# A scheduler that lays Fourier mixes later after their sines, and new shares for its four side chains: a vision-transformer layer on one core

## The chip, the core and the metric

The kernel runs on one core of one Trainium2 chip. The metric is the device time of one execution in microseconds (us), median of the runs of one comparison. The engines of the core are named as the profile names them: PE (TensorE; PEld is its weight loads), DVE (VectorE), ACT (ScalarE), POOL (GpSimd) and SP (SyncE, which here only issues DMAs). They run side by side and wait for each other through semaphores.

## What is computed

Sixteen images of 3 x 512 x 512 pixels are cut into 1024 patches of 768 values each. All numbers are float32.

```
h = patches @ W.T + b                              # tokens, width 256
x = layernorm(h);  q, k, v = split(x @ w_qkv)       # 8 heads of 32
k = sum over f = 1..256 of a_f*sin(f*k) + b_f*cos(f*k)   # element by element
h = h + softmax(q @ k.T / sqrt(32)) @ v @ w_out + b_out
x = layernorm(h)
h = h + mlp(x) + top-2 of 4 experts(x), weighted    # gates: softmax, top 2, softmax again
```

## The kernel before

The 256 Fourier terms of a key are not taken one by one. For a group of 8 rows of keys three tiles of 128 x 1024 are made: two "slow" waves `w` and one "fast" wave `f`. A DMA copies the angles into `w` (a shuffle on DVE copies them into `f`), POOL multiplies each row by its frequency (`turn`, line 953), and ACT takes the sine (line 963). Then PE **mixes**: sixteen matmuls on tiles of 64 x 32 combine the two slow waves with the coefficients (`mix`, line 987). The first eight read wave 0 and the next eight wave 1. DVE multiplies the result by the fast wave (`prod`, line 1001), and a matmul on tiles of 128 x 32 adds up what belongs together (`red`, line 1020). Each image has 32 such groups; all sixteen have 512.

Attention follows two rounds behind: scores on PE (`sT`, line 1085), exponentials on ACT (line 1100), and the weighing of the values on PE with tiles of 128 x 64 (`av`, line 1117). Then come a reciprocal and a product on DVE.

This fixed work is laid out in **rounds**: four groups of keys, and eight blocks of scores of one attention step (a pair of heads, half of the queries). Within a round ACT does twelve sines in one go, then loads the other table, then does eight exponentials: `sine` twice for group 0, twice for group 1, once for each of their fast waves, and the same again for groups 2 and 3. Eight rounds make an image, 130 rounds the whole. I call the stretch from the last `av` matmul of a round to the last mix of the next round the **sine phase**, and the stretch from there to its last `av` the **attention phase**.

All the rest is cut into pieces and fed to four **chains**, Python generators which yield the engine they want next: chain 0 keys, queries and values; chain 1 projection, gates and networks; chain 2 the small work on gate weights; chain 3 tokens and first norm of coming images. On PE nearly all of these pieces run on the full 128 x 128 array.

A planner, executed while the kernel is built, decides in which order the instructions stand on each engine. It keeps a modelled clock for every engine and a modelled time `done` for every result. `begin` gives the earliest start of a fixed step: the engine's clock, or the time of its dependencies plus `LAG` = 0.06. The loop `run` looks at the next fixed step on PE and at the pieces that want PE. A piece is laid if it can start early enough before the fixed step (`then - IDLE`, or `fixed - 2 * SWITCH` where the fixed step would go on in the tiling that PE already has), or if its chain is overdue (`due > 0`) and the fixed step would not go on in that tiling. `due` grows with the modelled cost of fixed PE work: for each chain `PACES` holds a share and a cap, and a piece of the chain takes its own cost off again. Other costs of the model: `SWITCH` = 0.18 for another tiling, a sine 0.96, a mix 0.86.

A mix depends on the sine of its slow wave 0 and on "sine late", which is set to the end of the sine of slow wave 1 less 0.1. The planner's clock decides the order alone: on the chip every instruction still waits on its semaphores.

Of the kernel before, what the change touches and what calls it, by code (L numbers as in the profile page):

```python
# [53 lines left out]


LAG, LANDS, TABLE, PER_COLUMN, SWITCH, IDLE = 0.06, 2.0, 1.28, 1.0 / 600, 0.18, 0.3
PACES = ((0.155, 2), (0.44, 2), (0, 0), (0.178, 2.6))

TILINGS = {"mix": (64, 32), "av": (128, 64), "red": (128, 32)}

@with_exitstack
def plain_path(ctx: ExitStack, tc: tile.TileContext, a: dict, out: bass.AP, verdict: bass.AP):
# [152 lines left out]
    clock = {e: 0.0 for e in (PE, ACT, DVE, POOL, SP)}  # L215
    queues = {e: {} for e in clock}
    done = {}
# [12 lines left out]
    def begin(engine, deps):  # L230

        if any(d not in done for d in deps):
            return None
        return max([clock[engine]] + [done[d] + LAG for d in deps])

    def retile(tiling):

        same = now["tiling"] == tiling
        now["tiling"] = tiling
        return 0.0 if same else SWITCH  # L240

    def together(at, queue):

        (cost, _, key, _), *rest = queues[PE][queue][:2]
        tiling = TILINGS.get(key[0])
        if tiling is None or now["tiling"] == tiling or not rest or rest[0][2][0] != key[0]:
            return at
        then = begin(PE, rest[0][1])
        return at + 2 * IDLE if then is None else max(at, then - cost)
# [6 lines left out]
    def side_tile(name):  # L256

        i = chains[now["chain"]]["bank"] = banks(now["chain"])[0][1]
        return side.tile([P, 512], FP, tag=f"side{i}", name=name)
# [91 lines left out]
    def lay(engine, queue):  # L351
        cost, deps, key, action = queues[engine][queue].pop(0)
        at = begin(engine, deps)
        if engine == PE:
            cost += retile(TILINGS.get(key[0]))
        clock[engine] = at + cost
        done[key] = clock[engine]
        if engine == PE:
            for ch, (pace, most) in zip(chains, PACES):
                ch["due"] = min(ch["due"] + pace * cost, most)  # L360
        action()

    def heads(engine):
        for rank, (name, steps) in enumerate(queues[engine].items()):
            at = begin(engine, steps[0][1]) if steps else None
            if at is not None:
                yield at, rank, name
# [30 lines left out]
    def run():  # L398

        while True:  # L400
            soonest = others(clock[PE])
            fixed = min(heads(PE), default=None)
            then = fixed and together(fixed[0], fixed[2])
            follows = fixed and TILINGS.get(queues[PE][fixed[2]][0][2][0]) == now["tiling"] != None
            pieces = [
# [307 lines left out]
    def gates(b, half, late=False):  # L713
# [20 lines left out]
        now["stream"] += 2 * P  # L734
        now["piece"] = TILINGS["red"]
        yield ACT, 0.25
# [17 lines left out]
    def networks(b, half, late=False):  # L754
# [29 lines left out]
        def second_of_experts(u, e1):  # L784
            yield GO
            ps = side_tile("e2p")
            now["piece"] = TILINGS["av"]
            now["stream"] -= 512
# [397 lines left out]
    for b in range(B):  # L1186
# [6 lines left out]
        late = b == B - 1  # L1193
# [799 lines left out]
```

## Time and profile before

| | before |
|---|---|
| time, median of three runs | 4168.1 us (4166.77 to 4168.17) |
| span of the profiled execution | 4169.3 us |
| PE, ACT, POOL, DVE busy | 97%, 79%, 77%, 68% |
| granted TensorE clock, mean | 0.993 |
| one image in the steady part | 250.6 us |

The last row is the distance between the first PE instructions after the last `av` matmul of one image's rounds and the next one's (1153.84 to 1404.47 us). Matmuls of PE are pipelined and their ends are modelled, so that a PE that stands still inside a group of matmuls is shown as busy. The chain of waits and the timeline tell more than the share.

### The profile page before, as it was taken

To read this page: it belongs to the slowest core of one execution; us is meant where nothing else is said; L and a number is where in the kernel's file an instruction comes from. 1 tells how busy PE (TensorE), PEld (TensorE's weight loads), DVE (VectorE), ACT (ScalarE), POOL (GpSimd) and SP (SyncE) were. 2 spreads that over 40 slices of the span, in tenths; PEclk is the share of its full clock that TensorE was granted. 3 is DMA by queue.
4 is the path that set the end of the run, shared out by engine and by line. 5 is a ranking of instruction groups with operands and counts; after the bars stand their busy time and mean duration, and the time that the engine had idled before them with its cause. 6 is when DMAs were issued, how large, how long until landed. Compare 5 with 4: busy or idle time off the path is not lost.

```text
span 4169.3 us, 67564 instructions
## 1 busy us (share of the span) xinstructions
PE 4027.4 (97%) x22753; PEld 1766.4 (42%) x22753; DVE 2830.2 (68%) x4172; ACT 3286.3 (79%) x3939; POOL 3195.8 (77%) x2323
## 2 busy tenths in 40 slices
PE   6889999999999999999999999999999999999998
PEld 4324344443434445344444444444444444443334
DVE  4667767677676776767767677776767767677652
ACT  2688888788787888878788888788788788888873
POOL 3988877778787887878787787888778787787850
PEclk9999999999999999999999999999999999999999
DMA  7988878888787887978878878887887978878740
GB/s 223 263 241 222 243 200 223 238 218 247 207 232 219 239 235 210 244 211 224 247 209 238 221 225 225 228 241 209 234 228 219 251 211 239 219 211 226 197 138 16
DMA packets 587478, 914.27 MB, mean 219 GB/s; under 512 B 58828, under 2 KB 177524, under 8 KB 587124
## 3 DMA queue, kind: packets, MB, share of 16 engines
q1 hardware_dynamic: 580880, 906.98, 78.7%
q8 instruction: 184, 3.01, 0.3%
q10 hardware_dynamic: 6244, 2.88, 0.3%
q14 instruction: 170, 1.39, 0.1%
HBM read 758.64 MB, written 150.99 MB: 218 GB/s over the span
## 4 chain that ended last, share of the span: by engine, by line
PE 74%; ACT 10%; DVE 6%; DMA 5%; issue 3%; SPq 2%; POOL 1%; ACTq 0%; DVEq 0%; POOLq 0%
PE av L1117 18%; PE sT L1085 11%; PE kan L987 9%; PE tok L263 6%; PE e3p L263 5%; PE red L1020 5%; PE e1p L263 5%; ACT w L963 4%; DMA w<-ud 3%; PE s1p L263 3%; PE q L263 2%; PE v L263 2%; PE proj L263 2%; DVE f L1001 2%; PE k L263 2%
## 5 line engine op out<-in xcount | busy, mean ns | idle before, releaser
L953 POOL TENSOR_TENSOR w<-w,lane 128x1024 int32<-128x1024 int32 x1024 | 1926.1, 1896 | 444.4 <-DMA w<-ud 298.6
L1100 ACT ACTIVATE es<-sT 128x1024 f32<-128x1024 f32 x1024 | 1033.0, 1022 | 550.0 <-PE av L1117 339.8
L953 POOL TENSOR_TENSOR f<-f,lane 128x1024 int32<-128x1024 int32 x512 | 971.0, 1896 | 251.2 <-DVE f L938 157.5
L963 ACT ACTIVATE w<-w 128x1024 f32<-128x1024 int32 x1024 | 1021.1, 1048 | 42.1 <-POOL w L953 39.1
L1117 PE MATMUL av<-es,v 128*64 128x512 f32 x4096 | 965.1, 602 | 1.0 <-DVE rc L1162 1.0
L1143 DVE RECIPROCAL rc<-av 128x256 f32<-128x256 f32 x256 | 434.0, 1730 | 702.6 <-PE av L1117 702.6
L1085 PE MATMUL sT<-q,k 128*128 128x512 f32 x2048 | 691.7, 449 | 42.0 <-DVE f L1001 20.2
L1001 DVE TENSOR_TENSOR f<-kan,f 128x1024 f32<-128x1024 f32 x512 | 608.5, 1218 | 159.8 <-ACT f L963 123.7
L938 DVE STREAM_SHUFFLE f<-src 128x1024 int32<-128x1024 int32 x512 | 673.0, 1353 | 0.7
L987 PE MATMUL kan<-w,coef 64*32 64x512 f32 x8192 | 623.9, 600 | 39.5 <-ACT w L963 35.6
L1085 PEld LDWEIGHTS sT<-q,k 128*128 128x128 f32 x2048 | 346.0, 189 | 440.5 <-issue 219.0
L963 ACT ACTIVATE f<-f 128x1024 f32<-128x1024 int32 x512 | 516.1, 1048 | 2.6 <-POOL f L953 2.6
L1117 PEld LDWEIGHTS av<-es,v 128*64 128x64 f32 x4096 | 258.5, 136 | 563.2 <-issue 498.2
L263 PE MATMUL tok<-wt,x 128*128 128x256 f32 x1536 | 362.3, 387 | 16.9 <-DMA w1s<-in_sW 13.6
L263 PEld LDWEIGHTS tok<-wt,x 128*128 128x128 f32 x1536 | 288.7, 192 | 110.8 <-issue 34.7
L987 PEld LDWEIGHTS kan<-w,coef 64*32 64x32 f32 x8192 | 127.9, 105 | 375.2 <-ACT w L963 222.5
L1020 PE MATMUL red<-f,pack 128*32 128x512 f32 x2048 | 273.6, 604 | 1.5 <-DVE f L1001 1.3
L263 PE MATMUL e1p<-hT,w1e 128*128 128x512 f32 x480 | 233.2, 608 | 0.4 <-ACT e L799 0.4
L462 ACT ACTIVATE hn<-h,less,rstd 128x256 f32<-128x256 f32 x256 | 143.8, 591 | 51.6 <-POOL less L454 51.2
L963 ACT ACT_TABLE_LOAD x128 | 164.2, 1283 | 22.4 <-DMA w<-ud 20.2
L1150 DVE TENSOR_TENSOR aT<-av,rc 32x512 f32<-32x512 f32 x256 | 176.1, 688 | 6.4
L1231 ACT ACT_TABLE_LOAD x128 | 164.2, 1283 | 2.2
(125 smaller groups left out, 3746.7 us busy)
## 6 DMA issues: line engine op xcount, KB each, us to landing
w<-ud SPq DMA_DIRECT2D x2048, 256.0 KB
q<-qd SPq DMA_DIRECT2D x512, 128.0 KB
k<-kd SPq DMA_DIRECT2D x128, 512.0 KB
x<-in_xT SPq DMA_DIRECT2D x128, 384.0 KB
ud<-u SPq DMA_DIRECT2D x64, 512.0 KB
ud<-ui SPq DMA_DIRECT2D x64, 512.0 KB
src<-ud SPq DMA_DIRECT2D x512, 64.0 KB
qd<-qhi SPq DMA_DIRECT2D x64, 256.0 KB
```

What stands on the lines that cost most here:

```text
L263: nc.tensor.matmul(out=out, lhsT=lhsT, rhs=rhs, start=start, stop=stop)
L938: nc.vector.stream_shuffle(w, sources[g // 8].rearrange("p r n -> p (r n)"), [4 * (g % 8) + i // 8 for i in range(32)],)
L953: nc.gpsimd.tensor_tensor(w, w, f.to_broadcast([P, N]), ALU.mult)
L963: nc.scalar.activation(x, w, AF.Sin, scale=TURN * 2.0**-32)
L987: nc.tensor.matmul(out=ps[ds(64 * j + 32 * blk, 32), ts(r, 512)], lhsT=coef[ts(r, 64)].rearrange("p e f j -> p (e f j)"), rhs=w[ts(r, 64), ...
L1001: nc.vector.tensor_mul(w, kan.pop(g), w)
L1020: nc.tensor.matmul(out=rows_of_pair[p][ts(2 * i + r, 32), :], lhsT=pack[:, ds(PACK0 - 16 * (k % 2) - 2 * (k // 2), 32)], rhs=prod[:, ts(r, ...
L1085: nc.tensor.matmul(out=ps[:, ts(s, 512)], lhsT=k4[:, 2 * s + kc // 4, ts(kc % 4, P)], rhs=q4[:, s, :], start=True, stop=True,)
L1100: nc.scalar.activation(es, scores.pop(kc), AF.Exp, scale=SCALE)
L1117: nc.tensor.matmul(out=acc[0][ts(s, 64), :], lhsT=v[:, kc, p % NPAIR, ds(HD * s, 64)], rhs=es[:, ts(s, 512)], start=(kc == 0), stop=(kc == ...
L1143: nc.vector.reciprocal(rc[0][:, part], acc[0][:, part])
L1150: nc.vector.tensor_mul(aT[ds(64 * (i % 2) + HD * s, HD), i // 2, ts(qb, 512)], acc[0][ds(96 * s, HD), :], rc[0][ds(HD + HD * s, HD), :],)
```

## The change

Every dependency of a step whose name is "sine" or "sine late" now counts in the planner as available 0.4 after the modelled end of the sine instead of 0.06. Only mixes, and the product with the fast wave on DVE, have such dependencies. The planner therefore takes the mixes to be possible 0.34 later than before, so that a piece of a chain may still be laid ahead of one. The second part sets new shares for the chains: chain 0 gets 0.25 with a cap of 1.5 (0.155 and 2 before), chain 1 gets 0.42 with a cap of 1 (0.44 and 2), chain 3 gets 0.16 with a cap of 2 (0.178 and 2.6). No instruction is added or removed; the order on the engines changes.

```diff
 LAG, LANDS, TABLE, PER_COLUMN, SWITCH, IDLE = 0.06, 2.0, 1.28, 1.0 / 600, 0.18, 0.3
-PACES = ((0.155, 2), (0.44, 2), (0, 0), (0.178, 2.6))
+PACES = ((0.25, 1.5), (0.42, 1), (0, 0), (0.16, 2))
 
 TILINGS = {"mix": (64, 32), "av": (128, 64), "red": (128, 32)}
+LATE, DOUBTFUL = 0.4, ("sine", "sine late")
...
         if any(d not in done for d in deps):
             return None
-        return max([clock[engine]] + [done[d] + LAG for d in deps])
+        return max([clock[engine]] + [done[d] + (LATE if d[0] in DOUBTFUL else LAG) for d in deps])
```

## The prediction

> **What bounds the kernel now.** I read the page first: the shares, the chain that ended last, the groups.
>
> ```profile
> PE 4027.4 (97%) x22753; PEld 1766.4 (42%) x22753; DVE 2830.2 (68%) x4172; ACT 3286.3 (79%) x3939; POOL 3195.8 (77%) x2323
> ...
> PE 74%; ACT 10%; DVE 6%; DMA 5%; issue 3%; SPq 2%; POOL 1%; ACTq 0%; DVEq 0%; POOLq 0%
> ...
> L987 PE MATMUL kan<-w,coef 64*32 64x512 f32 x8192 | 623.9, 600 | 39.5 <-ACT w L963 35.6
> ```
>
> PE seems full, yet only 74% of the chain is PE's, so some of its "busy" is standing still. The list of waits says for whom the mixes stand:
>
> ```profile
> PEld kan L987 <- ACT w L963: 222.5, 341, 4.6
> ...
> ACT w L963 <- POOL w L953: 39.1, 22, 10.0
> ```
>
> (us in total, times, longest). The mixes wait for sines; the sines hardly wait for POOL. How long such a stall is, the timeline of one sine phase shows, ACT first, then PE (start, length, instructions):
>
> ```profile
> 1220.75 1.04 ACT L963 ACTIVATE w<-w 128x1024 f32<-128x1024 int32 x1
> 1221.70 0.66 ACT L781 ACTIVATE e<-e1p,b1e 128x512 f32<-128x512 f32 x1
> 1222.27 2.94 ACT L963 ACTIVATE w<-w 128x1024 f32<-128x1024 int32 x3
> 1225.11 1.98 ACT L963 ACTIVATE f<-f 128x1024 f32<-128x1024 int32 x2
> ```
>
> ```profile
> 1219.43 1.98 PE L263 MATMUL e1p<-hT,w1e 128*128 128x512 f32 x4
> 1222.41 0.50 PE L263 MATMUL wb<-w,sel 20*128 20x512 f32 x1 [1.00 <-ACT e L781]
> 1222.84 3.48 PE L987 MATMUL kan<-w,coef 64*32 64x512 f32 x32
> 1226.25 1.06 PE L1020 MATMUL red<-f,pack 128*32 128x512 f32 x8
> ```
>
> Two mixes take 3.48 us here, because the last slow sine ends at 1225.2. Undisturbed they take 1.88, and one alone 1.02; the list of the chain, piece by piece, has both:
>
> ```profile
> 1531.67 0.57 PE lnT L267 x4
> 1532.24 1.37 PE kan L987 x16
> ...
> 1536.20 1.02 PE kan L987 x16
> 1537.22 1.00 PE red L1020 x8
> ...
> 1562.41 1.88 PE kan L987 x32
> ```
>
> So a mix costs 1.88 - 1.02 = 0.86, and its change of tile shape 1.02 - 0.86 = 0.16.
>
> Last, busy time by stretch for the eight rounds from 1153.84 to 1404.47 us, one image. In the sine phases, together 105.4 us, ACT is busy 104.1 and PE 104.0. In the attention phases, together 145.2, PE is busy 143.6 and ACT 101.0. The attention phase is PE's alone: a piece put there lengthens it. The sine phase belongs to both: it ends when PE is through its pieces or about 1.1 us after the last slow sine (in the round with no chain work on ACT that sine ended 9.5 us into the phase, which took 10.6).
>
> **What the Trainium skill says.** "TensorEngine Tiling (Array Packing)", Key Properties: a change of the tiling mode drains the array; this trace agrees, with the 0.16 above. "PSUM — Partial Sum Buffer", Engine vs sequencer instructions: ACT and DVE work strictly first in, first out, and matmuls start and complete in program order. So a mix laid too early holds all that stands behind it on PE, as the red at 1226.25 shows. "Perfetto Trace Analysis", Identifying the Most-Contended Engine: matmul busy time doesn't tell how near PE is to its limit; the 97% beside 74% of the chain agrees.
>
> **The change, part by part.** I compared the orders of instructions of the two built kernels. Every engine has the same instructions. So the streaming work is the same, and the change moves three terms.
>
> 1. *Changes of tile shape on PE.* Counted in the orders: 1832 before, 1762 after, most of them where a weighing group is followed by work on the full array (404 before, 356 after). 70 x 0.16 = **11 us less**. All are on PE, which sets the end.
>
> 2. *Standing still in sine phases.* Before, I take the length of a phase less its work: four mixes 3.41, its pieces (at the streaming time of a 128x512 float32 matmul, 1.71 for four instructions, e.g. k), 0.16 per change. Over an image that leaves 7.1 us in the first half of the run and 5.2 in the second (the planner settles into two different periodic patterns, both near 250.5 us an image). After, there is one pattern throughout. Its pieces in sine phases shrink from 64 to 58.6 us an image. For its eight rounds I add up the pieces, and take the later of PE's end (work plus 0.1, or 0.35 where the mixes stand in three or more groups, as measured in like rounds) and the last slow sine plus 1.1 (9.5 plus the chain work ahead of it on ACT, 0.3 to 0.6 a piece by its row):
>
> | round | mixes in groups of | pieces | PE's end | ACT's end | phase |
> |---|---|---|---|---|---|
> | 1 | 2, 2 | 6.8 | 11.0 | 10.6 | 11.0 |
> | 2 | 1, 1, 2 | 6.0 | 10.5 | 13.1 | 13.1 |
> | 3 | 2, 1, 1 | 8.1 | 13.0 | 12.2 | 13.0 |
> | 4 | 1, 1, 2 | 4.7 | 9.2 | 11.2 | 11.2 |
> | 5 | 2, 1, 1 | 8.2 | 13.1 | 11.8 | 13.1 |
> | 6 | 2, 2 | 10.2 | 14.4 | 13.4 | 14.4 |
> | 7 | 2, 2 | 7.2 | 11.4 | 11.2 | 11.4 |
> | 8 | 2, 1, 1 | 7.3 | 12.0 | 11.1 | 12.0 |
>
> The sum is 99.2. The same rule gives 104.6 for the first pattern of before, where 105.4 was measured, so I correct to 100.0; less work of 92.4, that is 7.6 us of standing still. In rounds 1, 3 and 5 to 8 PE's pieces set the end. Rounds 2 and 4 wait more than before, because no piece was ready in the planner: the margin can only be filled with what there is.
>
> 3. *Standing still in attention phases.* Before, with 11.95 us of fixed work a round (eight scores, eight weighings, two reds): 6.8 us an image in the first pattern, 7.5 in the second. The worst rounds there are one with no piece between the scores (2.1) and one whose pieces of gates and first norm stand between the weighings (2.3). After, the pieces are spread more evenly, 1.7 to 6.8 us a round, where before they ran from 0.1 to 7.7. By like rounds I get 6.2 for the eight. The pieces that leave the sine phases, 5.4 us an image, lengthen these phases in full; the sine phases are shorter by as much (105.4 to 100.0).
>
> Sum of 2 and 3: 13.8 after, 13.9 and 12.7 before. Such a walk is good to about 1.5 us an image, so I count no change. What remains is term 1: 4168 - 11 = 4157, taken as **4156**.
>
> The margin also reaches the product on DVE. DVE is busy 68%, and the product waits for its mix anyway; I cost it at nothing. A later mix frees its wave tiles later, and behind these wait a DMA, POOL's turn and the sine four groups on. POOL has 23% of slack, and all that ACT waited for POOL's slow waves is 39 us: between 0 and some 20 us, of which I take 0. Start and end hold the same work: the first eight rounds have equal pieces in both phases, and the 34 pieces behind the last `av` stand in the same order.
>
> **The rivals.**
> *The sine stalls go.* The chip's sines may lag the planner's times in ways that my walk doesn't see, and the margin is made for these. For: the 222 us in the list of waits; by the starts of their matmuls 77 of the 512 mixes stand over 0.35 us between their two halves, and all of them 64 us. Against: ACT is full in these phases, so a mix can't come sooner than its sine, and the gain needs pieces to fill with. If half the standing in sine phases (6 of before, 14 images) goes on top of term 1, it is 11 + 42 = 53 us less: 4115.
> *The attention phase pays.* The 5.4 us an image leave phases where ACT may hide them and enter phases where nothing does. If the sine phases give back only half, the loss is 2.7 x 14 = 38 us, less term 1: 4168 + 27 = 4195, slower than before. For: a straight line through the rounds of before gives 0.40 us of round per us of pieces in the sine phase and 0.90 in the attention phase, so that moving 69 us, as counted over the run, costs 35. Against: term 1, and that the pieces taken were partly in rounds where PE set the end.
>
> **How the numbers follow.** My forecast 0.46, the first rival 0.22, the second 0.32. Within the forecast, ±1 us an image spreads it by about 14 us: some 0.7 of it lies faster than 0.2% (8.3 us), the rest within. The second rival's low end, where the sine phases give back three quarters, lies within too (0.05). Faster 0.22 + 0.32 = 0.54, same 0.14 + 0.05 = 0.19, slower 0.32 - 0.05 = 0.27. The range goes from the first rival's 4115 to the second's 4195.
>
> **What would show it.** After: the mean of the mixes' group and its busy sum fall a little, an image of the steady part takes about 249.7 us, and the sine phases of one image add up to about 100 us and the attention phases to about 150. If the sine phases stay at 105, the second rival holds; if PE's wait for slow sines halves and an image falls under 247, the first. A slower run with more of ACT's waits for POOL's slow waves would mean that late mixes starve the loads, which I put at nothing.

## The result, and the profile after

| | before | after |
|---|---|---|
| time, median of four runs each (lowest, highest) | 4168.0 us (4166.8, 4168.2) | 4200.4 us (4196.1, 4209.1) |
| ratio after to before, 95% interval | | 1.0081 (1.0063 to 1.0098) |
| span of the profiled execution | 4169.3 us | 4207.2 us |
| mean of one steady image (twelve) | 250.4 us | 252.6 us |
| its sine phases, its attention phases | 104.3, 146.1 us | 99.5, 153.1 us |

The kernel is slower by 32 us; the forecast had it faster by 12. Every ratio, here and below, is against runs of the kernel before made beside the kernel in question; their medians lie between 4168.0 and 4171.9 us. The page of the changed kernel, in the order in which I read before (lines of the code have moved down by one):

```profile
PE 4032.8 (96%) x22753; PEld 1781.7 (42%) x22753; DVE 2816.1 (67%) x4172; ACT 3291.0 (78%) x3939; POOL 3193.9 (76%) x2323
...
PE 75%; ACT 8%; DMA 5%; DVE 5%; issue 3%; POOL 2%; SPq 1%; ACTq 0%; DVEq 0%; POOLq 0%
...
L988 PE MATMUL kan<-w,coef 64*32 64x512 f32 x8192 | 634.8, 612 | 61.1 <-ACT w L964 55.2
```

Nothing here names a loss of 32 us. PE is busy 5 us more, and the mixes' group costs 11 us more and has 22 us more of idle time before it, behind slow waves `w`. The list of waits of the changed kernel (us in total, times, longest) is no plainer:

```profile
PEld kan L988 <- ACT w L964: 238.4, 344, 4.7
...
ACT hn L463 <- POOL less L455: 56.9, 28, 13.0
...
ACT w L964 <- POOL w L954: 36.1, 18, 10.5
```

The last line matters because the prediction named it as the sign that late mixes starve the loads: it was 39.1 before and is 36.1 now. So they don't. The middle line was 51.2 before, under the same names:

```profile
ACT hn L462 <- POOL less L454: 51.2, 30, 13.0
```

It looks unchanged, and it is where the answer lies. To find it I cut both traces into the same stretches, each from the first PE instruction after an `av` or mix to the next such point:

| us | start, to the end of the first attention step | seven full rounds | next image | twelve steady images | last but one image | last image and rest |
|---|---|---|---|---|---|---|
| before | 179.4 | 191.2 | 248.9 | 3004.9 | 246.1 | 298.8 |
| after | 179.2 | 197.1 | 244.7 | 3031.3 | 253.8 | 301.0 |
| difference | -0.2 | +5.9 | -4.2 | +26.4 | +7.7 | +2.2 |

Most of it is in the steady images. There the sine phases became shorter by 4.8 us an image, as forecast, and the attention phases longer by 7.0. So the time is lost where the forecast expected nothing but the pieces that moved. For one steady image, busy time of each engine in the eight attention phases, first before, then after (us; the columns after the length are PE, its loads, DVE, ACT, POOL; the first line of after is round 1's phase):

```profile
sum 145.24, PE 143.60 PEld 59.90 DVE 86.94 ACT 100.97 POOL 124.68; mean PE 17.95 PEld 7.49 DVE 10.87 ACT 12.62 POOL 15.58
```

```profile
3187.74:3212.14 24.40, 20.73 (x122) 10.84 (x114) 14.99 (x35) 16.71 (x24) 22.57 (x22) 1.00 1.01 262
...
sum 154.02, PE 148.80 PEld 63.13 DVE 97.17 ACT 106.57 POOL 137.74; mean PE 18.60 PEld 7.89 DVE 12.15 ACT 13.32 POOL 17.22
```

PE was idle 145.24 - 143.60 = 1.6 us before and 154.02 - 148.80 = 5.2 after, and 3.7 of these 5.2 lie in round 1. The timeline of the end of that phase shows why, first PE, then ACT, then POOL (start, length, instruction, and in brackets how long the engine stood idle and for whom):

```profile
3204.70 2.80 PE L1118 MATMUL av<-es,v 128*64 128x512 f32 x12
3209.28 1.08 PE L1118 MATMUL av<-es,v 128*64 128x512 f32 x4 [1.78 <-ACT es L1101]
3212.14 1.06 PE L988 MATMUL kan<-w,coef 64*32 64x512 f32 x8 [1.78 <-ACT w L964]
```

```profile
3205.17 0.21 ACT L646 ACTIVATE gp<-gp 128x16 f32<-128x16 f32 x1
3207.72 0.60 ACT L463 ACTIVATE hn<-h,less,rstd 128x256 f32<-128x256 f32 x1 [2.34 <-POOL less L455]
3208.22 1.00 ACT L1101 ACTIVATE es<-sT 128x1024 f32<-128x1024 f32 x1
3209.13 0.59 ACT L463 ACTIVATE hn<-h,less,rstd 128x256 f32<-128x256 f32 x1
3209.73 1.28 ACT L964 ACT_TABLE_LOAD   x1
3211.03 1.06 ACT L964 ACTIVATE w<-w 128x1024 f32<-128x1024 int32 x1
```

```profile
3201.92 3.75 POOL L954 TENSOR_TENSOR w<-w,lane 128x1024 int32<-128x1024 int32 x2
3205.75 0.23 POOL L451 TENSOR_SCALAR rstd<-mv 128x4 f32<-128x4 f32 x1
3206.06 1.04 POOL L452 TENSOR_TENSOR rstd<-rstd,mhalf 128x4 f32<-128x4 f32 x1
3207.17 0.24 POOL L454 TENSOR_SCALAR less<-mv 128x4 f32<-128x4 f32 x1
3207.49 0.20 POOL L455 TENSOR_TENSOR less<-less,rstd 128x4 f32<-128x4 f32 x1
```

`hn` is the last step of a token's first norm, a piece of chain 3: ACT computes h times `rstd` plus `less`, and POOL makes these two small tiles in four steps of 1.7 us together. But the steps stand in POOL's queue behind two wave multiplications of 1.9 us, which nobody needs yet (the sines that read them start some 15 us after they end). On ACT `hn` stands ahead of the round's last exponential and of the first sines. So a wait for POOL that belongs to a side chain holds the last exponential (the last `av` stands 1.78 us) and all that follows it on ACT: the table, the first sine, the first mix. The 1.78 us for which that mix stands are not a second loss of this size: the mix has to wait for the table and the sine in any case, and where `hn` is hardly late it stands 1.70 (experiment 4). "PSUM — Partial Sum Buffer" of the Trainium skill, Engine vs sequencer instructions, says that ACT works strictly first in, first out; the trace agrees: ACT is idle 2.34 us up to 3207.7 while the next exponential can't pass.

The list of waits of PE's matmuls shows how often this happens; the list of before has no wait of `av` for `es`:

```profile
PE av L1118 <- ACT es L1101: 11.7, 7, 3.6
```

Six of the seven lie in the last six of the twelve steady images. In the first six, `hn` stands just behind the last exponential and ahead of the table load. There no `av` waits, but the first mix does; ACT and then PE at the longest of these:

```profile
1689.15 0.60 ACT L463 ACTIVATE hn<-h,less,rstd 128x256 f32<-128x256 f32 x1 [2.21 <-POOL less L455]
1692.17 3.37 PE L988 MATMUL kan<-w,coef 64*32 64x512 f32 x16 [3.79 <-ACT w L964]
```

At these twelve places `hn` waits 0.35 to 4.2 us, 19 us in all. In the kernel before, no `hn` waits for POOL ahead of a last exponential or of the table for the sines.

### The profile page after: what moved, and what is told of

Read it like the earlier page. It is cut to its first block, busy times and chain, and to the rows that moved or that the text cites. A ratio compares the mean times of both kernels' runs of the same rounds, so it can differ in the third digit from the quotient of the medians.

```text
span 4207.2 us, 67639 instructions
## 1 busy us (share of the span) xinstructions
PE 4032.8 (96%) x22753; PEld 1781.7 (42%) x22753; DVE 2816.1 (67%) x4172; ACT 3291.0 (78%) x3939; POOL 3193.9 (76%) x2323
## 4 chain that ended last, share of the span: by engine, by line
PE 75%; ACT 8%; DMA 5%; DVE 5%; issue 3%; POOL 2%; SPq 1%; ACTq 0%; DVEq 0%; POOLq 0%
PE av L1118 17%; PE sT L1086 11%; PE kan L988 11%; PE tok L264 6%; PE red L1021 5%; PE e3p L264 5%; PE e1p L264 5%; ACT w L964 3%; PE s1p L264 3%; DMA w<-ud 2%; PE k L264 2%; PE v L264 2%; PE proj L264 2%; ACT es L1101 2%; PE q L264 2%
## 5 line engine op out<-in xcount | busy, mean ns | idle before, releaser
L964 ACT ACTIVATE w<-w 128x1024 f32<-128x1024 int32 x1024 | 1020.3, 1048 | 37.5 <-POOL w L954 36.1
L1118 PE MATMUL av<-es,v 128*64 128x512 f32 x4096 | 965.7, 602 | 12.6 <-ACT es L1101 11.7
L1086 PE MATMUL sT<-q,k 128*128 128x512 f32 x2048 | 682.7, 447 | 39.7 <-ACT es L1101 30.8
L988 PE MATMUL kan<-w,coef 64*32 64x512 f32 x8192 | 634.8, 612 | 61.1 <-ACT w L964 55.2
L264 PE MATMUL tok<-wt,x 128*128 128x256 f32 x1536 | 359.5, 385 | 15.4 <-DMA x<-in_xT 13.2
```

What stands on the lines that cost most here:

```text
L264: nc.tensor.matmul(out=out, lhsT=lhsT, rhs=rhs, start=start, stop=stop)
L964: nc.scalar.activation(x, w, AF.Sin, scale=TURN * 2.0**-32)
L988: nc.tensor.matmul(out=ps[ds(64 * j + 32 * blk, 32), ts(r, 512)], lhsT=coef[ts(r, 64)].rearrange("p e f j -> p (e f j)"), rhs=w[ts(r, 64), ...
L1086: nc.tensor.matmul(out=ps[:, ts(s, 512)], lhsT=k4[:, 2 * s + kc // 4, ts(kc % 4, P)], rhs=q4[:, s, :], start=True, stop=True,)
L1118: nc.tensor.matmul(out=acc[0][ts(s, 64), :], lhsT=v[:, kc, p % NPAIR, ds(HD * s, 64)], rhs=es[:, ts(s, 512)], start=(kc == 0), stop=(kc == ...
```

## The experiments

**Theory.** The new shares put the last tokens of an image and their first norm into round 1's attention phase; `hn` there waits behind POOL's queue, and what stands behind `hn` on ACT (last exponential, sines) waits with it, and so do `av` and mix on PE. **Rivals.** The margin itself makes mixes late. Or the wait is there but harmless, and the loss is the pieces that moved into attention phases.

**1. Each part alone.** First the new shares with the old margin, then the margin with the old shares.

```diff
 # shares alone
-return max([clock[engine]] + [done[d] + (LATE if d[0] in DOUBTFUL else LAG) for d in deps])
+return max([clock[engine]] + [done[d] + LAG for d in deps])
 # margin alone
-PACES = ((0.25, 1.5), (0.42, 1), (0, 0), (0.16, 2))
+PACES = ((0.155, 2), (0.44, 2), (0, 0), (0.178, 2.6))
```

> The new shares of the chains alone, sines at the old margin of 0.06. Theory (in the first round of every image two normalising steps of the first norm stand ahead of the last exponential on ACT and wait for POOL, so the last weighing and the next sines come late): the built order has 31 such steps with seven exponentials of their attention step done, against 25 in the changed kernel and 14 before, so 4185 to 4205. Rival 1 (pieces moved from sine phases to attention phases cost half their time): only 22 of the 69 us move, 66 changes of tile shape fewer, so 4165 to 4172. Rival 2 (late mixes starve the loads of the waves): no margin, so about 4157.

> The margin of 0.4 alone, with the old shares. Theory (normalising steps ahead of the last exponential): only 12 such steps, so as before or better by its 37 changes of tile shape fewer, 4155 to 4170. Rival 1 (pieces in attention phases): here 56 us of pieces move out of the attention phases into the sine phases, so it gains half of that and the tile shapes, about 4134. Rival 2 (late mixes starve the loads): 4190 or more, since the margin is whole.

Shares alone: 4199.5 us, 1.0072 (1.0059 to 1.0085) times before: nearly all of the loss, and its steady images take 3027.8. In all twelve of them `hn` waits ahead of the last exponential, 1.2 to 3.9 us each. Margin alone: 4310.6, 1.0338 (1.0325 to 1.0352), which no theory had. Nearly all of its loss is in four of the twelve steady images, which take 283 to 290 us instead of about 250. Three rounds of one of them, one after the other, each line with length and busy time of PE, loads, DVE, ACT, POOL:

```profile
992.90:1022.80 29.90, 29.77 (x186) 15.81 (x184) 19.32 (x30) 24.74 (x29) 23.69 (x17) 1.00 0.90 233
1022.80:1053.00 30.20, 24.68 (x155) 7.81 (x153) 15.23 (x32) 24.39 (x31) 11.87 (x20) 0.94 0.12 35
1053.00:1134.40 81.40, 68.22 (x288) 33.67 (x286) 41.96 (x60) 32.38 (x39) 41.64 (x24) 0.96 0.77 219
```

The third takes 81 us, with nearly twice the PE instructions of the others, while its ACT has only a third more to do. I read it so: with the margin more pieces go early, but chain 0's old share of 0.155 lets the keys of the next image fall behind, until the fixed steps have no keys to take and the planner runs the chains alone. That PE then waits on them piece after piece is in the trace:

```profile
1104.32 3.78 PE L264 MATMUL q<-hnT,wq 128*128 128x512 f32 x4 [7.35 <-DVE qlo L566]
```

So the two parts aren't additive: the shares alone have already lost the time, and the margin needs one of the new shares. That it is chain 0's 0.25 is not shown; no run changes that share alone.

**2. `hn` behind the exponential.** In the changed kernel, the first norm's `hn` is issued behind the last exponential of an attention step. Only ACT's order changes.

```diff
-            nc.scalar.activation(hn[:, t, :], h[:, t, :], AF.Identity, ...)
+            if behind and fixed and fixed[0][2][0] == "exp":
+                held_back.append(norm)      # norm() is the activation
+            else:
+                flush()
+                norm()
...
+            if kc == NT - 1:                # behind the step's last exponential
+                flush()
```

> The changed kernel with one thing moved: normalising steps of the first norm that the planner lays between exponentials of an attention step are issued behind the last of these; the order on all other engines is the same. Theory: the stall of PE ahead of the last weighings of the first round goes (about 2.5 us an image), but the first sines still stand behind steps that wait for POOL, and part of it comes back in the next sine phase; 4175 to 4190. Rivals 1 and 2: no difference, 4196 to 4209.

4227.2 us, 1.0134 (1.0118 to 1.0150): slower still. The timeline of the same place, PE and then ACT, tells why:

```profile
3228.18 3.65 PE L1134 MATMUL av<-es,v 128*64 128x512 f32 x16
3234.61 3.37 PE L1002 MATMUL kan<-w,coef 64*32 64x512 f32 x16 [2.78 <-ACT w L978]
```

```profile
3229.36 1.02 ACT L1115 ACTIVATE es<-sT 128x1024 f32<-128x1024 f32 x1 [0.52 <-PE av L1134]
3231.09 1.09 ACT L470 ACTIVATE hn<-h,less,rstd 128x256 f32<-128x256 f32 x2 [0.71 <-POOL less L461]
3232.20 1.28 ACT L978 ACT_TABLE_LOAD   x1
3233.50 1.06 ACT L978 ACTIVATE w<-w 128x1024 f32<-128x1024 int32 x1
```

The exponential is on time and the sixteen `av` run through. But now the sines stand behind the same `hn`, and the first mix waits 2.78. One queue was only traded for another, and the edit also lengthened another sine phase of the image by 1.9 us (13.6 against 11.7).

**3. `hn` without its wait.** All orders stay, but the first norm's `hn` reads neither `rstd` nor `less`: the first normalisation is left out of the result, and POOL's steps remain. The same edit on the kernel before is the control. `hn` itself becomes shorter too (0.41 instead of 0.59 us).

```diff
-                hn[:, t, :], h[:, t, :], AF.Identity, bias=less[:, one], scale=rstd[:, one]
+                hn[:, t, :], h[:, t, :], AF.Identity, scale=1.0
```

> The changed kernel with the first norm's normalising steps reading neither mean nor deviation: they copy h (the first normalisation is left out; POOL still works out both), so that these steps on ACT no longer wait for POOL. The order of all engines is the same. Theory: the first round of an image loses its stall of about 2.5 us and the second round's sine phase falls from 13.1 to about 12 us, 12 to 13 images, so 4150 to 4165. Rivals 1 and 2: POOL's delay isn't the cause, 4190 to 4205.

> The control of the run before this: the kernel before the change with the first norm's normalising steps reading neither mean nor deviation (the first normalisation is left out), all orders as they were. Theory (only the new order brings those steps ahead of an exponential while POOL is late): little to gain, 4155 to 4168, against the 33 us that the same edit took from the changed kernel. If the wait on POOL costs the kernel before as much, the theory falls: about 4135.

After without the wait: 4166.9 us, 0.9992 (0.9986 to 0.9999) times before, 33 us faster than after (37 by the two ratios). Before without it: 4165.6, 0.9983 (0.9977 to 0.9990), 6 us faster than before. The steady images now take 2998.4 us in both kernels. The place, again PE and ACT:

```profile
3177.43 3.65 PE L1119 MATMUL av<-es,v 128*64 128x512 f32 x16
3182.37 1.06 PE L989 MATMUL kan<-w,coef 64*32 64x512 f32 x8 [1.28 <-ACT w L965]
```

```profile
3178.00 0.41 ACT L463 ACTIVATE hn<-h 128x256 f32<-128x256 f32 x1
3178.62 1.02 ACT L1102 ACTIVATE es<-sT 128x1024 f32<-128x1024 f32 x1 [0.21 <-PE av L1119]
3179.96 1.28 ACT L965 ACT_TABLE_LOAD   x1
3181.26 1.06 ACT L965 ACTIVATE w<-w 128x1024 f32<-128x1024 int32 x1
```

No `av` stands, and the first mix waits 1.28 us, until the table is loaded and the first sine is done. Of the steady loss of 26.4 us none is left against the control, so what was taken away is the loss. The rival that blames the moved pieces falls, for these pieces are still where they were.

But two things were taken away, the wait and 0.18 us of each `hn`, and the control shares only the edit, not its effect. In the changed kernel four `hn` of each image stand at this place, from just ahead of the last exponential to the fourth sine, where ACT is what PE waits for; four times 0.18 in twelve images is an estimate of 9 us. In the kernel before, `hn` also stands among sines, but a sine phase with four of them (1153.84 to 1167.55 us) takes 13.7 us with the edit and without it. So of the 33 us this run can't say how much is the wait alone. The next experiment can, for it leaves `hn` as it is.

**4. POOL's small steps first.** In the changed kernel, each wave multiplication is held until two more are due or its own sine is, so that small steps pass up to two of them. Only POOL's order changes. The second run does so only from the 17th group on, the third does that to the kernel before.

```diff
-            nc.gpsimd.tensor_tensor(w, w, f.to_broadcast([P, N]), ALU.mult)
+            turns.append(((g, j), lambda: nc.gpsimd.tensor_tensor(w, w, f.to_broadcast([P, N]), ALU.mult)))
+            turn_now(2)             # second and third run: turn_now(2 if g >= 16 else 0)
```

> The changed kernel with POOL's order alone altered: each multiplication of a wave is issued up to two such multiplications later, so that the small steps of the norms pass two of them (3.8 us). Nothing is left out. Theory (the norm's small steps on POOL stand behind two wave multiplications that they need not wait for): the normalising steps come up to 3.8 us sooner, the first round's attention phase falls from 24 to about 22 us, 4165 to 4180. If the waves then come too late for the sines, it shows as ACT waiting for POOL's slow waves (37 us now) and eats the gain, 4195 or more. Rival 1 (pieces moved into attention phases): no change, 4196 to 4209.

> The changed kernel with POOL's order altered as before (small steps pass two wave multiplications), but only from the seventeenth group of keys on, so that the start, where that order cost 15 us, stays as it is. Theory: the steady part took 3008 us with it against 3031, so 20 to 25 us less than the changed kernel, 4172 to 4180. If the gain in the steady part belonged to that one execution: 4195 or more.

> The control for POOL's order: the kernel before the change with small POOL steps ahead of two wave multiplications from the seventeenth group on. Theory: its norms hardly wait for POOL where it matters, so 4158 to 4172, against 20 to 25 us gained in the changed kernel. A gain of 20 us here too would say that POOL's order is a general cost and not what the change brought out.

First: 4197.6 us, 1.0060 (1.0047 to 1.0073), no gain in sum. But its steady images take 3008.5, 23 us less than after, and its first stretch 194.0 instead of 179.2; probably POOL has no backlog there, and holding a multiplication only makes it late. Second: 4188.0, 1.0045 (1.0031 to 1.0059), 12 us faster than after (15 by the ratios), steady images 3007.4; part of the gain was lost at the start (2.4 and 0.9 us in the first two stretches) and in the image behind it (250.3 against 244.7).

The 24 us that the steady images gain over after lie where the theory has them: 19 in round 1's attention phases and 5 in round 2's sine phases, and the other phases are as they were. In the last six images `hn` still stands ahead of the last exponential, but waits 0.23 to 0.26 us for POOL instead of 1.3 to 4.2; all sixteen `av` run through, and the first mix stands about as long as in after:

```profile
3199.55 1.06 PE L998 MATMUL kan<-w,coef 64*32 64x512 f32 x8 [1.70 <-ACT w L974]
```

This is the run that carries the theory: nothing is left out of the computation, `hn` has its full length, and some 24 of the 26.4 us are gone. With the 9 us estimated for the shorter `hn` it also makes up the 33 of experiment 3. The wait shrank in the list as well; its line in the second run and then in the third:

```profile
ACT hn L462 <- POOL less L454: 23.4, 17, 13.0
```

```profile
ACT w L974 <- POOL w L960: 56.8, 49, 5.4
...
ACT hn L462 <- POOL less L454: 27.1, 12, 13.0
```

Third: 4210.6, 1.0097 (1.0081 to 1.0112), 39 us slower than before, and far from the 4158 to 4172 expected. There the wait for `less` went down as well (51.2 to 27.1) and no gain came of it. Sines now wait 57 us for their multiplications instead of 39; whether that is the loss wasn't traced, so POOL's order is no free gain by itself. The totals misled me: before, `hn` waited for `less` nearly as long in sum, but ahead of the early exponentials of a round, never ahead of the last one or of the table for the sines.

**5. The planner told of it.** The chain counts as ready 3.0 later behind POOL's four steps.

```diff
             nc.gpsimd.tensor_tensor(less, less, rstd, ALU.mult)
+            chains[now["chain"]]["ready"] += 3.0
```

> The changed kernel, whose planner also takes the norm's mean and deviation on POOL to be ready 3 us later than its clock says, so that the steps that read them are laid later. Theory: in the steady pattern the first norm's steps move out of the attention phase of the token round into the sine phases of the next but one, and nothing stands before the last exponential but what is ready; 4140 to 4165. Rival 1: the pieces shift back by 56 us into sine phases, half of that gained, 4172.

4226.0 us, 1.0124 (1.0110 to 1.0139), a miss. The plan settled into another pattern, which stands still 129.6 us in the sine phases of the steady part where after has 82.8. It says nothing on the wait; a planner of this kind gives a new order to every edit.

**6. One share back, and the margin for mixes only.** Chain 1 gets its old share again; separately, the margin is kept from the product on DVE; last, both together with the second run of 4.

```diff
 # one share back
-PACES = ((0.25, 1.5), (0.42, 1), (0, 0), (0.16, 2))
+PACES = ((0.25, 1.5), (0.44, 2), (0, 0), (0.16, 2))
 # mixes only
-(LATE if d[0] in DOUBTFUL else LAG)
+(LATE if engine == PE and d[0] in DOUBTFUL else LAG)
```

> The changed kernel with chain 1's old share (0.44, cap 2) and all else new. Its order has 122 us of pieces more in sine phases than the changed kernel, 48 changes of tile shape more, and the first norm's steps between the first exponentials of the first round, not before the last. Rival 1 (pieces in attention phases cost half their time): 4200 - 61 + 8 = 4147. Theory: the stall before the last exponential goes, but steps that wait for POOL still stand before others, 4165 to 4185.

> The changed kernel with the margin for mixes alone, not for the product with the fast wave on DVE. Theory of the start (in the second full round the margin lets two copies of a query piece on DVE go before the round's last product, which holds a bank of scores and lets PE cool): the stretch of the first seven full rounds falls from 197 to about 191.5 us, the steady part keeps its waits on POOL: 4190 to 4197. If the start's loss isn't from the product's place: no change, 4196 to 4209.

> Chain 1's old share, the margin for mixes alone, and small POOL steps ahead of two wave multiplications from the seventeenth group on; all else as in the changed kernel. If the three causes add up: 4172 with the old share, less 5 at the start, less 10 to 15 for the first round's attention phase, 4150 to 4158, under both kernels. If they don't, because the new plan puts other steps behind POOL: 4165 to 4180.

One share back: 4172.5 us, 1.0000 (0.9992 to 1.0008), steady images 3003.3, within the 4165 to 4185 that the theory gave. In this plan no `hn` waits ahead of a last exponential or of the sines' table. In round 1 it stands among the first exponentials, where it waits up to 2.1 us, e.g.

```profile
1170.45 0.60 ACT L462 ACTIVATE hn<-h,less,rstd 128x256 f32<-128x256 f32 x1 [0.87 <-POOL less L454]
```

That isn't free: round 1's attention phase, with hardly a piece between its scores, still stands 2.6 to 6.4 us. But the plan stands less in sine phases (some 50 us over the steady part against 83), so its gain can't be put down to the moved `hn` alone. Mixes only: 4197.9, 1.0069 (1.0055 to 1.0082), steady as after (3027.7), but the start's seven rounds take 191.4, as before, instead of 197.1. All together: 4222.9, 1.0126 (1.0111 to 1.0142), a miss: this plan stands more than 5 us in round 2's sine phase of each image.

The start's 5.9 us come from that product. In all kernels with the margin on it those seven rounds take 195.8 to 200.8 us, in all without it 191.1 to 192.5. DVE at that place, before and then after:

```profile
217.38 2.35 DVE L1001 TENSOR_TENSOR f<-kan,f 128x1024 f32<-128x1024 f32 x2
219.65 0.68 DVE L564 CAST qhi<-q 128x512 fp32r<-128x512 f32 x1
```

```profile
218.78 0.68 DVE L565 CAST qhi<-q 128x512 fp32r<-128x512 f32 x1
219.49 0.69 DVE L566 TENSOR_TENSOR qlo<-q,qhi 128x512 fp32r<-128x512 f32 x1
220.10 1.21 DVE L1002 TENSOR_TENSOR f<-kan,f 128x1024 f32<-128x1024 f32 x1
```

With the product due later in the planner, a query's split of 1.4 us is put ahead of the round's last product. PE then has gaps (2.16 us busy of the 4.0 from 219 us on), and after them its clock is halved. Windows from 223.5 us in after and in the run with the margin for mixes only (length, PE, loads, DVE, ACT, POOL, granted clock):

```profile
223.50:230.00 6.50, 5.32 (x16) 1.67 (x18) 1.21 (x3) 1.02 (x1) 6.50 (x4) 0.50 1.06 324
```

```profile
223.50:230.00 6.50, 6.50 (x31) 2.07 (x31) 4.31 (x7) 3.57 (x4) 6.50 (x4) 1.00 1.06 303
```

At half the clock, and with 1.2 us of standing, PE gets through 16 matmuls where it else does 31.

## Why the prediction was wrong

**Term 1, fewer changes of tile shape, held as a count.** Nothing measured it alone. Without the wait (and with the shorter `hn`) both kernels' steady images take 2998.4 us. By the walk, after then stands 13.8 us an image, and the 70 changes saved are 0.7; that before stood about as much less is consistent with it, no more.

**Term 2, the sine phases, was right.** Round by round, the walk and what the twelve images show on average:

| round | 1 | 2 | 3 | 4 | 5 | 6 | 7 | 8 | sum |
|---|---|---|---|---|---|---|---|---|---|
| walk | 11.0 | 13.1 | 13.0 | 11.2 | 13.1 | 14.4 | 11.4 | 12.0 | 99.2 |
| measured | 11.1 | 13.2 | 13.1 | 11.2 | 13.3 | 14.5 | 11.5 | 11.7 | 99.5 |

Standing still was 6.9 us where 7.6 was forecast. Part of this agreement is luck: the 13.2 of round 2 holds half a us of slower clock that followed the stalls (last section), which the walk knew nothing of; with POOL's small steps first it is 12.8, and without the wait 12.2. The first rival, by which the sine stalls go, fell: PE's loads wait 238 us for slow waves instead of 222.

**Term 3, the attention phases, is the step that failed.** "By like rounds I get 6.2 for the eight" took what rounds of before with as many pieces had stood. Measured are 3.8, 0.4, 0.5, 1.6, 0.5, 0.5, 1.2 and 1.0, in sum 9.6: round 1 alone is 3.8. No round of before is like it, for none there has an `hn` that waits for POOL ahead of its last exponential or of the sines' table. I had the orders of all engines and walked the sine phases on PE and ACT, but took the attention phases to be "PE's alone" and didn't walk ACT and POOL through them. The mis-sized term is this one, by 3.4 us an image and some 41 over twelve; the pieces' own part was right. About half of the 3.4 is the wait: 1.6 go with POOL's small steps first, 1.8 in the run without the wait. The other half stays in both, so "like rounds" was too low in itself, and which rounds make it so wasn't traced. That the run without the wait stands 7.8 in attention and 6.0 in sine phases, together the very 13.8 forecast, is luck: the two are off by 1.6 each, in opposite directions.

**The second rival, "The attention phase pays", had the number (4195) and not the cause.** It let the sine phases give back only half; they gave back nearly all (4.8 of 5.4). The straight line through rounds of before, which spoke for it, couldn't see a single wait either.

**"I cost it at nothing", the margin on the product, was wrong by 5 to 6 us, and so was "Start and end hold the same work".** The work was the same, but at the start its order on DVE was not. That the last image but one takes 7.7 us longer is explained only in part: some 2 go with the wait (251.7 in the second run of experiment 4). With one share back it takes 246.6, as before, but the shares alone have 254.1 and the margin alone 256.4; the cause of the rest is open.

**The bound for POOL, "between 0 and some 20 us, of which I take 0", looked at the wrong wait.** Sines waiting for slow waves didn't move. POOL's queue cost through the norm's small steps, which the prediction never named.

From before to after the profiled executions lose 38 us (the medians 32): 26.4 in the steady images, of which some 24 are the wait and the clock that follows it; 5.9 at the start, for the product; 7.7 in the last image but one, about 2 of them the wait; 2.2 at the end, less 4.2 in the image ahead of the steady ones. The rest up to the forecast is the gain of term 1, which no run shows. A version that keeps the computation and is faster than before was not among the runs. Moving the four small steps off POOL's queue wasn't tried.

## What to carry to other kernels

A planner or a reordering that looks at one engine's stalls can put a cheap instruction of a side chain ahead of an urgent one on an engine with an in-order queue; before counting such an edit as free, walk each moved instruction on its engine: whom does it wait for, what stands ahead of that producer in its own queue, and who stands behind the waiter. The total of a wait in a list doesn't answer this: "`hn` waits for `less`" was 51 us before and 57 after, and the edit that took the wait away gained 6 us in one kernel and 33 in the other (some 24 of them by the wait), because of what stood behind it. Moving the waiter behind one urgent step only handed the wait to the next (experiment 2). Letting the producer's small steps pass got the time back in the steady part of this kernel, but lost 39 us in the one before, so look at both ends of each wait.

## What the runs showed of the hardware

I had not expected the clock to take part. "TensorE: Matmul & The Clock Gate" of the Trainium skill, What's actually happening, says that the array falls to half its clock after an idle window of about 3.4 us and comes back after a busy one. Here no single stall is that long: PE stands 1.78, works 1.08, and stands 1.78 again, and then the clock is halved for 3.1 us or more (the granted clock is the third number from the end):

```profile
3207.50:3213.20 5.70, 2.14 (x13) 0.35 (x12) 2.79 (x2) 5.45 (x7) 5.46 (x12) 1.00 0.85 192
3213.50:3216.60 3.10, 3.02 (x20) 1.03 (x28) 2.34 (x5) 2.42 (x5) 3.10 (x2) 0.50 0.79 211
3217.00:3222.00 5.00, 5.00 (x30) 2.25 (x15) 2.63 (x3) 5.00 (x8) 5.00 (x3) 1.00 0.83 266
```

So a window that is busy for 2.14 us of 5.7 was enough. After has 22 such stretches of half clock, 112 us in all, and before 11 with 59; in the steady images it is 41 us against 7, and in the run without the wait none. They cost less than half their length. In the last six images round 2's sine phase takes 13.1 to 13.2 us with a stretch of 3.4 us and 13.6 with one of 6.8; with POOL's small steps first, where five of these six have none, it takes 12.4 in those five. ACT is busy in nearly all of it (12.4 of 13.1 us), so a slower PE hides behind ACT in part. By such differences the half clock makes up some 6 of the 26.4 us lost in the steady images (an estimate, round by round), and it goes when the wait goes.
